# Attention and a feed-forward net side by side on one core: the first values in seven products, weight sums and the first rotation on GpSimd

## Chip, core and metric

The kernel runs on one core of a Trainium2 chip. The metric is the device time of one execution in microseconds (us). Before the change the median of three runs is 2091.97 us (2091.55 to 2092.16). One execution was also recorded by the profiler; the times of single instructions below come from that one. The engines are called PE (TensorE's matmuls; PEld are its weight loads), DVE (VectorE), ACT (ScalarE), POOL (GpSimd) and SP (SyncE, which here only issues DMAs).

## The reference

Sixteen batches of 512 tokens with 256 features. Everything is float32.

```python
def attn(x, wq, wk, wv, wo):                    # x: (16, 512, 256), 8 heads of 128
    q = rope(jnp.einsum('bim,mhd->bhid', x, wq))
    k = rope(jnp.einsum('bim,mhd->bhid', x, wk))
    v = jnp.einsum('bim,mhd->bhid', x, wv)
    s = jnp.einsum('bhid,bhjd->bhij', q, k) / 128
    s = s - 1e30 * mask                         # mask: i < j
    p = jax.nn.softmax(s, axis=-1)
    return jnp.einsum('bhid,hdm->bim', jnp.einsum('bhij,bhjd->bhid', p, v), wo)

def ffn(x, k0, k1, k2, s0, s1, s2):             # weights are +1 or -1
    h = jnp.concatenate([x, -x], axis=-1)
    h = jax.nn.relu(s0 * conn_dense(k0, h)) * 2
    h = jax.nn.relu(s1 * conn_dense(k1, h)) * 2
    return s2 * conn_dense(k2, h)

xn = layernorm(x)
out = x + attn(xn, wq, wk, wv, wo) + ffn(xn, k0, k1, k2, s0, s1, s2)
```

`rope` turns each head's vector by an angle that grows with the position: with the vector's two halves a and b, it gives a cos - b sin and a sin + b cos.

## The kernel before

**Tiling.** A batch's normalized tokens lie transposed in SBUF (`xnT`: features on the partitions, in two chunks of 128; tokens along the row, in four blocks of 128). A projection to 512 tokens is therefore two matmuls of 128x512 per head, or, for the values, where tokens are the output's rows, four products of 128x256 for each block of 128 tokens and each group of four heads (`project_v_directly`, L383: the sum over the two feature chunks, for two halves of the columns). One float32 matmul appears in the trace as two matmul records and two weight loads.

**Seven products.** A product of a 2x2 block matrix with a 2x2 block matrix needs eight block products; the kernel does most projections with seven, by a scheme of Strassen's kind (`seven_products`, L427). The weights' blocks A11, A12, A21 and A22 lie in places of `w7_sb` (queries and keys) and `wv7_sb` (values), beside three sums S1, S2 and S4, which `sum_w7` (L687) makes in four subtractions, the last of which replaces A21. Before them `scale_w7` (L680) scales the four blocks; for the values that is one instruction, the negation of A22, since the other scales are 1. Sums of the tokens' blocks are in `tt` (`make_ts`, L363, four subtractions a batch). Of the seven products two go to a PSUM tile `pa`, then two to a PSUM tile `pb`. ACT copies pa to `ca` and pb to `cb` in SBUF. The fifth product adds to pa, ACT copies one half of that to `cu`, the sixth adds to pb, the seventh to pa. Three additions on DVE then give the four blocks of the result. The tiles pa and pb come from a pool of three PSUM tiles (`ps_mm`), which also serves the direct projections and the feed-forward net; a tile is free again when its last reader is done.

**Rotation.** `rotate` (L395) has ACT swap the two halves of a head's vector from PSUM or SBUF into `sw` (two copies of 64x512), DVE multiply the source by the cosine, and then `engine` multiply sw by the sine (L411) and add the two (L413). For head 0 that engine is DVE (L879), for all others GpSimd.

**Stages.** The order on PE, SP and GpSimd is the program's order. In the opening (L874 to L884) that holds for DVE and ACT too; later a scheduler orders these two. The opening: normalize the first batch from `x_first`, transpose it on PE, make `tt` and the net's scales (`make_scales`, whose last result `c_sb` scales the tokens in `split_xn`), project head 0's q and k directly, split the tokens into two rounded halves (`split_xn`, ACT makes xh, DVE makes xl), and turn the net's first weights from bits into numbers (`make_w0`, L221: ACT makes `kb`, DVE `w0_sb`, for two chunks). Then come 128 slots, one per batch and head, each with the scores and softmax of its head (`score_row`), the projection of the next head's q and k, the attention product of the head before (`attend`), and a part of the net. The first slot (`first_slot`, L711) projects the values of the first batch's heads 0 to 3 directly, then head 1's q and k directly, then alternates score rows of head 0 with tiles of the net's first layer (`ffn0`). The later slots of the first batch make the sums of weights for what follows, on GpSimd; in the slot of head 4 these are the sums for the values of heads 0 to 3 (L868), which the next batch is the first to use.

**Loads.** SP issues them: the first tokens, head 0 and 1's wq, the cosine, the first group of the value weights (`load_wv(0)`, two DMAs), the scales s, k0, and then the rest. ACT issues half of the first tokens, wk of heads 0 and 1, and the sine.

The lines around the first values:

```python
        project_v_directly(0, 0)                       # L713
        rest(project_qk_directly(1, nc.gpsimd))        # L714
```

Of the kernel before, what the change touches and what calls it, by code (L numbers as in the profile page):

```python
# [9 lines left out]
F32 = mybir.dt.float32  # L10
# [12 lines left out]
def kernel(  # L23
# [36 lines left out]
    nc = tc.nc  # L60
    P = 128
    B, T, M = x.shape
# [3 lines left out]
    NT = T // P  # L66
    NM = M // P
# [14 lines left out]
    ps_mm = ctx.enter_context(tc.tile_pool(name="ps_mm", bufs=3, space=bass.MemoryType.PSUM))  # L82
# [17 lines left out]
    def load_x_sum(b):  # L100

        t = xpool.tile([P, NT, M], F32, tag="x_sum", name=f"x_sum_{b}", bufs=1)
        nc.sync.dma_start(t, by_chunks(x, b))
        return t
# [12 lines left out]
    A11, A12, A21, S1, S2, A22, S4 = range(7)  # L117
    WQ0, WQ1, WK0, WK1 = A11, A12, A21, A22
    NG = HD // (VH * D)
    VN = VH * D // 2  # L120
    wv7_sb = wpool.tile([P, 7, NG, VN], F32, tag="wv7", name="wv7_sb")
# [131 lines left out]
    xns, zxs, bounces, xnTs, halves, tts = {}, {}, {}, {}, {}, {}  # L253
# [58 lines left out]
    def tokens(t, m):  # L312
        return t[:, :, m].rearrange("p i c a -> p i (c a)")
# [9 lines left out]
    def carry_xn_out(b):  # L323
        bounces[b] = carry_out(zxs.pop(b).rearrange("p j m c a -> p j (m c a)"), "bounce_x", b)
# [50 lines left out]
    vts, qks, probs, pTs, oTs = {}, {}, {}, {}, {}  # L375
# [4 lines left out]
    def new_v(b, gv):  # L380
        vts[b, gv] = work.tile([P, NT, VH * D], F32, tag="v", name=f"v_{b}_{gv}")

    def project_v_directly(b, gv):  # L383
        new_v(b, gv)
        for c in range(NT):
            pv = ps_mm.tile([P, T], F32, tag="mm", name=f"pv_{b}_{gv}_{c}")
            for i, places in enumerate(((A11, A12), (A21, A22))):
                for m in range(NM):
                    nc.tensor.matmul(  # L389
                        pv[:, ts(i, VN)], tokens(xnTs[b], m)[:, c], wv7_sb[:, places[m], gv],  # L390
                        start=(i == 0 and m == 0), stop=(m == NM - 1), skip_group_check=True,
                    )
            nc.scalar.copy(vts[b, gv][:, c, :], pv)

    def rotate(src, name, g, engine, scale=1.0):  # L395


        sw = work.tile([P, T], F32, tag="sw", name=f"sw{name}_{g}")
        rt = work.tile([P, T], F32, tag=f"{name}T", name=f"{name}T_{g}")
        for to, half in ((sw[0:HALF, :], src[HALF:D, :]), (sw[HALF:D, :], src[0:HALF, :])):  # L400
            if scale == 1.0:
                nc.scalar.copy(to, half)  # L402
            else:
                nc.scalar.mul(to, half, scale)
        if scale == 1.0:
            nc.vector.tensor_tensor(rt, src, cos_sb, ALU.mult)
        else:
            nc.vector.scalar_tensor_tensor(rt, src, scale, cos_sb, ALU.mult, ALU.mult)
        qks.setdefault(g, []).append(rt)
        yield  # L410
        engine.tensor_tensor(sw, sw, sin_sb, ALU.mult)  # L411
        yield
        engine.tensor_tensor(rt, rt, sw, ALU.add)  # L413

    def project_qk_directly(g, engine):

        for name, places, scale in (("q", (WQ0, WQ1), Q_SCALE), ("k", (WK0, WK1), K_SCALE)):
            pq = ps_mm.tile([P, T], F32, tag="mm", name=f"p{name}_{g}")
            for m in range(NM):
                nc.tensor.matmul(  # L420
                    pq, w7_sb[:, places[m], ts(g, D)], tokens(xnTs[0], m),
                    start=(m == 0), stop=(m == NM - 1),
                )
            rest(rotate(pq, name, g, engine, scale))
            yield
# [60 lines left out]
    def project_v(b, gv, t):  # L486


        if t == 0:
            new_v(b, gv)  # L490
        vt = vts[b, gv]

        def product(out_, place, right, **marks):
            nc.tensor.matmul(  # L494
                out_, right[:, t], wv7_sb[:, place, gv], skip_group_check=True, **marks
            )

        for sums in seven_products(f"v_{b}_{gv}_{t}", b, product):
            if sums is None:
                yield  # L500
        nc.vector.tensor_tensor(vt[:, t, :VN], *sums[0], ALU.add)
        nc.vector.tensor_tensor(vt[:, t + 2, :VN], *sums[1], ALU.add)
        nc.vector.tensor_tensor(vt[:, t : t + 3 : 2, VN:], *sums[2], ALU.add)
        yield
# [165 lines left out]
    def rest(*gens):  # L670
        for gen in gens:
            for _ in gen:
                pass
# [6 lines left out]
    def scale_w7(w, i, scale1, scale2, raised=None):  # L680


        place, scale = ((A22, -scale2), (A21, scale2), (A11, scale1), (A12, scale1))[i]
        if scale != 1.0:
            behind(nc.scalar.mul(w[place], w[place], scale), raised)

    def sum_w7(w, reduced=None, engine=nc.vector):  # L687
        for out_, a, c in (
            (S1, A21, A22), (S2, S1, A11), (S4, A12, S2), (A21, A11, A21)
        ):  # L690
            tied = reduced if engine is nc.vector else None
            behind(engine.tensor_tensor(w[out_], w[a], w[c], ALU.subtract), tied)  # L692

    def w7_qk(h0, h1):
        return [w7_sb[:, i, h0 * D : h1 * D] for i in range(7)]

    def scale_w7_qk(h0, h1, i, raised):
        scale_w7(w7_qk(h0, h1), i, Q_SCALE, K_SCALE, raised)
# [6 lines left out]
    def make_w7_v(gv, reduced, raised, engine):  # L705
        w = [wv7_sb[:, i, gv] for i in range(7)]
        for i in range(4):
            scale_w7(w, i, 1.0, 1.0, raised)
        sum_w7(w, reduced, engine)

    def first_slot():  # L711
        l0 = [ffn0(0, f) for f in range(NF0)]
        project_v_directly(0, 0)  # L713
        rest(project_qk_directly(1, nc.gpsimd))  # L714
        for ic in range(NT):
            reduced, raised = score_row(0, ic)
            scale_w7_qk(2, 4, ic, raised)
            rest(l0[ic])
        sum_w7(w7_qk(2, 4), reduced, nc.gpsimd)
        turn(0, reduced)  # L720
        rest(*l0[NT:])
        make_w1(0, reduced, raised)
        load_w1(0, 0)
        for gv in range(1, NG):
            make_w7_v(gv, reduced, raised, engine=nc.gpsimd)
# [98 lines left out]
    def slot(g):  # L824
        b, h = divmod(g, H)
        load_w1(b, h)
        if h == 3:
            x_sums[b] = load_x_sum(b)
        if b + 1 < B:
            if h == 4:  # L830
                carry_xn_out(b + 1)
            if h == 5:
                carry_xn_back(b + 1)
        qk = project_qk(g + 1) if g + 1 < N_SLOTS else iter(())
        tile = ffn1(b, h - 1)
        v = iter(())
        if h in (2, 3):
            v = project_v(b, 1, h - 2)
        elif h == H - 1 and b + 1 < B:
            v = project_v(b + 1, 0, 0)  # L840
        some(qk, 1)
        for ic in range(NT):
            reduced, raised = score_row(g, ic)
            between_rows(b, h, ic, reduced, raised)
            if ic == 0:
                some(qk, 1)
                rest(ffn2(b, h - 2))
                some(qk, 1)
            else:
                some(tile, 4)  # L850
                if ic > 1:
                    some(qk, 1)
            if ic == 2:
                some(v, 1)
        rest(qk)
        turn(g, reduced)
        some(v, 1)
        project_o(g - 2)
        rest(v)
        rest(tile)  # L860
        attend(g - 1)
        if b == 0:
            make_w1(h, reduced, raised)
        if g == 2:
            make_w7_qk(6, H, reduced, raised, engine=nc.gpsimd)
        elif g == 3:
            make_w7_qk(0, 2, reduced, raised, engine=nc.gpsimd)
        elif g == 4:  # L868
            make_w7_v(0, reduced, raised, engine=nc.gpsimd)

    E = mybir.EngineType
    with tc.manual_schedule(engines={E.PE, E.SP, E.Pool}):
        with tc.manual_schedule(engines={E.DVE, E.Activation}):
            layernorm(0, x_first)  # L874
            transpose_first_xn()
            for i in range(4):
                make_ts(0, i)
            make_scales()
            q = project_qk_directly(0, nc.vector)  # L879
            next(q)  # L880
            split_xn(0, 0)
            rest(q)
            split_xn(0, 1)
            make_w0()  # L884
        first_slot()
        for g in range(1, N_SLOTS + 2):
            (slot_of_head_0, slot_of_head_1, slot)[min(g % H, 2)](g)
# [52 lines left out]
```

## Time and profile before

| what | value |
|---|---|
| median of three runs | 2091.97 us |
| the profiled execution | 2090.79 us |
| its span, first to last instruction | 2089.0 us |
| granted PE clock, mean | 0.999 |
| instructions | 30263 |
| bytes moved by DMA | 284.33 MB, 136 GB/s |

How to read it: a line of the trace in order of time gives the start (us from the span's beginning), the duration, the engine, the line of the kernel, the operation, what it writes `<-` what it reads, the shapes, and how many neighbours of one kind are merged (x4). In square brackets stands how long the engine was idle before it, and which instruction released it. Merged rows of one engine can overlap the next row by a little, because the ends of instructions include the way through the pipeline. A table of stretches gives for each stretch its length, and after the comma the busy time of PE, PEld, DVE, ACT and POOL with the number of their instructions.

The chain of waits, followed back from the end, goes through these lines of PE for most of the span:

| line | what | share |
|---|---|---|
| L648 | second layer of the net | 22% |
| L594 | sums into the output | 16% |
| L549 | probabilities times values | 13% |
| L511 | scores | 13% |
| L470 | q and k in seven products | 18% |
| L494 | values in seven products | 9% |
| L389 | values directly (first slot only) | 0.3% |

### The profile page before, as it was taken

What the parts mean: (1) busy time and instruction counts of PE and PEld (TensorE: products, weight loads), DVE (VectorE), ACT (ScalarE), POOL (GpSimd) and SP (SyncE); (2) the same over time, 40 slices, a digit from 0 to 9 for tenths busy, and PEclk for the clock granted to TensorE, in tenths of its full rate; (3) what the DMA queues carried; (4) which work ended last, traced back from release to release, by engine and by line L of the source; (5) the groups of instructions that cost most, each with busy time, mean ns of one, the idle gap of its engine ahead of it and who ended that gap; (6) DMA issues with size and microseconds to landing.
All of it is one profiled execution on the core that took longest, in us unless ns stands there. A gap on an engine that the chain in (4) does not pass through costs nothing.

```text
span 2089.0 us, 30263 instructions
## 1 busy us (share of the span) xinstructions
PE 2075.7 (99%) x9856; PEld 1730.4 (83%) x9856; DVE 1402.0 (67%) x3653; ACT 1086.6 (52%) x2419; POOL 1020.2 (49%) x1088
## 2 busy tenths in 40 slices
PE   8999999999999999999999999999999999999999
PEld 6888888888888888888888888888888888888887
DVE  7767666676766766667676676766667666676654
ACT  6655554555545555455554555555555554555543
POOL 5754545445454454444544455444544545545443
PEclk9999999999999999999999999999999999999999
DMA  6543545445444344543435444454453544534344
GB/s 182 164 145 118 159 116 147 132 123 149 126 144 136 122 138 126 149 139 119 146 114 163 125 136 135 120 159 116 137 151 112 152 116 141 157 117 137 106 139 129
DMA packets 162158, 284.33 MB, mean 136 GB/s; under 512 B 25168, under 2 KB 126544, under 8 KB 162000
## 3 DMA queue, kind: packets, MB, share of 16 engines
q1 hardware_dynamic: 160976, 281.34, 45.6%
q8 instruction: 78, 1.28, 0.3%
q10 hardware_dynamic: 1024, 1.05, 0.2%
q14 instruction: 80, 0.66, 0.1%
HBM read 178.00 MB, written 104.33 MB: 135 GB/s over the span
## 4 chain that ended last, share of the span: by engine, by line
PE 98%; DVE 1%; POOL 0%; issue 0%; ACT 0%; DMA 0%; POOLq 0%; DVEq 0%; ACTq 0%
PE ph L648 22%; PE y L594 16%; PE po L549 13%; PE s L511 13%; PE pa_qk L470 10%; PE pb_qk L470 8%; PE ph L633 6%; PE pa_v L494 5%; PE pb_v L494 4%; PE pv L389 0%; PE pq L420 0%; PE pk L420 0%; DVE p L514 0%; POOL w_sb L692 0%; DMA x_first<-in_L_attn_x_dram 0%
## 5 line engine op out<-in xcount | busy, mean ns | idle before, releaser
L522 POOL TENSOR_SCALAR p<-p,rl 128x128 f32<-128x128 f32 (+3 forms) x512 | 296.0, 583 | 733.2 <-DVE rl L521 730.0
L648 PE MATMUL ph<-h0h,w 128*128 128x512 f32 x1024 | 519.7, 507 | 0.0
L648 PE MATMUL ph<-h0l,w 128*128 128x512 f32 x1024 | 411.3, 402 | 0.0
L511 PE MATMUL s<-kT,qT 128*128 128x128 f32 (+3 forms) x1024 | 359.3, 432 | 0.2
L519 ACT ACTIVATE p<-p,least 128x128 f32<-128x128 f32 (+3 forms) x512 | 286.9, 561 | 123.6 <-DVE least L514 117.5
L411 POOL TENSOR_TENSOR swq<-swq,sin_sb 128x512 f32<-128x512 f32 x127 | 196.7, 1549 | 298.9 <-ACT swq L402 280.6
L530 DVE STREAM_TRANSPOSE z<-p 128x128 f32<-128x128 f32 (+3 forms) x512 | 241.8, 493 | 93.5 <-POOL p L522 89.8
L549 PEld LDWEIGHTS po<-pT,v 128*128 128x128 f32 x1536 | 271.1, 190 | 37.6
L549 PE MATMUL po<-pT,v 128*128 128x256 f32 (+1 forms) x1536 | 298.6, 344 | 0.0
L648 PEld LDWEIGHTS ph<-h0h,w 128*128 128x128 f32 x1024 | 193.1, 189 | 73.1 <-issue 26.9
L648 PEld LDWEIGHTS ph<-h0l,w 128*128 128x128 f32 x1024 | 193.3, 189 | 72.7 <-issue 26.8
L514 DVE CUSTOM_DVE_ANT_0 p<-s,causal 128x128 f32<-128x128 f32 (+3 forms) x512 | 244.2, 485 | 10.9 <-PE s L511 9.7
L402 ACT COPY swq<-q 64x512 f32<-64x512 f32 x252 | 156.3, 620 | 170.3 <-DVE q L480 168.9
L594 PE MATMUL y<-wo_sb,oT 128*128 128x256 f32 x1024 | 241.7, 379 | 0.0
L511 PEld LDWEIGHTS s<-kT,qT 128*128 128x128 f32 x1024 | 193.4, 189 | 33.6 <-POOL kT L413 0.5
L594 PEld LDWEIGHTS y<-wo_sb,oT 128*128 128x128 f32 x1024 | 193.9, 189 | 28.7
L445 ACT COPY ca_qk<-pa_qk 128x512 f32<-128x512 f32 x126 | 73.9, 587 | 275.2 <-PE pa_qk L470 275.2
L656 ACT ACTIVATE h1h<-ph 128x512 fp32r<-128x512 f32 x128 | 76.5, 597 | 250.7 <-PE ph L648 243.2
L521 DVE RECIPROCAL rl<-l 128x1 f32<-128x1 f32 x512 | 78.7, 154 | 145.5 <-ACT p L519 143.1
L413 POOL TENSOR_TENSOR kT<-kT,swk 128x512 f32<-128x512 f32 x127 | 169.2, 1332 | 0.1
L413 POOL TENSOR_TENSOR qT<-qT,swq 128x512 f32<-128x512 f32 x127 | 163.8, 1290 | 10.0
L411 POOL TENSOR_TENSOR swk<-swk,sin_sb 128x512 f32<-128x512 f32 x127 | 166.3, 1309 | 0.0
(107 smaller groups left out, 3497.9 us busy)
## 6 DMA issues: line engine op xcount, KB each, us to landing
bounce_p<-z SPq DMA_DIRECT2D x128, 640.0 KB, 2.9
pT<-bounce_p SPq DMA_DIRECT2D x512, 160.0 KB, 3.3
w<-w_dram SPq DMA_DIRECT2D x120, 512.0 KB, 5.2
x_sum<-in_L_attn_x_dram SPq DMA_DIRECT2D x16, 512.0 KB, 6.0
x<-in_L_attn_x_dram SPq DMA_DIRECT2D x60, 128.0 KB, 6.1
bounce_x<-zx SPq DMA_DIRECT2D x15, 512.0 KB, 6.7
xnT<-bounce_x SPq DMA_DIRECT2D x60, 128.0 KB, 5.9
out_dram<-x_sum SPq DMA_DIRECT2D x15, 512.0 KB, 4.5
```

What stands on the lines that cost most here:

```text
L411: engine.tensor_tensor(sw, sw, sin_sb, ALU.mult)
L413: engine.tensor_tensor(rt, rt, sw, ALU.add)
L470: nc.tensor.matmul(out_, w7_sb[:, place, ts(h, D)], right, skip_group_check=True, **marks)
L494: nc.tensor.matmul(out_, right[:, t], wv7_sb[:, place, gv], skip_group_check=True, **marks)
L511: nc.tensor.matmul(ps[:, :n], qT[:, ts(ic, P)], kT[:, :n], start=True, stop=True)
L514: reduced = nc.vector.tensor_tensor_reduce(out=p, in0=ps[:, :n], in1=causal[:, T - n :], scale=1.0, scalar=3e38, op0=ALU.add, op1=ALU.min, ...
L519: raised = nc.scalar.activation(p, p, AF.Exp, bias=least, scale=-1.0, accum_out=l)
L522: nc.gpsimd.tensor_scalar(p, p, rl, 1.0, ALU.mult, ALU.mult)
L530: behind(nc.vector.transpose(zs[:, :, block(ic, 0) : block(ic + 1, 0), :].rearrange("p j c a -> p c j a"), p.rearrange("p (c j a) -> p c j ...
L549: nc.tensor.matmul(po[:, (ics[0] - first) * P : (ics[-1] + 1 - first) * P], v[:, jc], pT[:, :, at[0] : at[-1] + 1 : max(at[-1] - at[0], 1) ...
L594: nc.tensor.matmul(ys[b][c // 2][:, c % 2, :], lhsT[:, ts(c, P)], rhs, start=(y_done[b][c] == 0 and c % 2 == 0), stop=(y_done[b][c] == N_Y ...
L648: nc.tensor.matmul(ph, w1s[b, f][:, c], h0s[b][i][:, c, :], start=(c == 0 and i == 0), stop=(c == NF0 - 1 and i == 1),)
```

## The change

The first batch's values of heads 0 to 3 are computed by `project_v`, in seven products for each half of the token blocks (t = 0: blocks 0 and 2; t = 1: blocks 1 and 3), as all other values are; `project_v_directly` is gone. The direct projection of head 1 is split: its q is projected between the two halves, its k after them. The scaled block and the sums of these value weights are made in the opening, after `make_scales`, with the four subtractions on GpSimd, and not in the slot of head 4. The two multiplications and two additions of head 0's rotation go from DVE to GpSimd, where they stand behind the sums.

```diff
-    def project_v_directly(b, gv):
-        new_v(b, gv)
-        for c in range(NT):
-            pv = ps_mm.tile([P, T], F32, tag="mm", name=f"pv_{b}_{gv}_{c}")
-            for i, places in enumerate(((A11, A12), (A21, A22))):
-                for m in range(NM):
-                    nc.tensor.matmul(
-                        pv[:, ts(i, VN)], tokens(xnTs[b], m)[:, c], wv7_sb[:, places[m], gv],
-                        start=(i == 0 and m == 0), stop=(m == NM - 1), skip_group_check=True,
-                    )
-            nc.scalar.copy(vts[b, gv][:, c, :], pv)
...
     def first_slot():
         l0 = [ffn0(0, f) for f in range(NF0)]
-        project_v_directly(0, 0)
-        rest(project_qk_directly(1, nc.gpsimd))
+        rest(project_v(0, 0, 0))
+        qk = project_qk_directly(1, nc.gpsimd)
+        next(qk)
+        rest(project_v(0, 0, 1), qk)
...
         elif g == 3:
             make_w7_qk(0, 2, reduced, raised, engine=nc.gpsimd)
-        elif g == 4:
-            make_w7_v(0, reduced, raised, engine=nc.gpsimd)
...
             make_scales()
-            q = project_qk_directly(0, nc.vector)
+            make_w7_v(0, None, None, engine=nc.gpsimd)
+            q = project_qk_directly(0, nc.gpsimd)
             next(q)
             split_xn(0, 0)
             rest(q)
```

`project_v`, which the first slot now calls, stood in the kernel before for the other values:

```python
    def project_v(b, gv, t):
        if t == 0:
            new_v(b, gv)
        vt = vts[b, gv]

        def product(out_, place, right, **marks):
            nc.tensor.matmul(
                out_, right[:, t], wv7_sb[:, place, gv], skip_group_check=True, **marks
            )

        for sums in seven_products(f"v_{b}_{gv}_{t}", b, product):
            if sums is None:
                yield
        nc.vector.tensor_tensor(vt[:, t, :VN], *sums[0], ALU.add)
        nc.vector.tensor_tensor(vt[:, t + 2, :VN], *sums[1], ALU.add)
        nc.vector.tensor_tensor(vt[:, t : t + 3 : 2, VN:], *sums[2], ALU.add)
        yield
```

In the changed kernel lines after L379 have smaller numbers: the copies ca, cb and cu are L433, L437 and L441, the three additions L489 to L491, the rotation's lines L390 to L401.

## The prediction

> **What bounds the kernel now.** I read the page's busy shares and its chain of waits first, then the first 31 us in order of time, because the change lies there, and last the busy time of stretches further on, to see what a shift at the start would meet.
>
> ```profile
> PE 2075.7 (99%) x9856; PEld 1730.4 (83%) x9856; DVE 1402.0 (67%) x3653; ACT 1086.6 (52%) x2419; POOL 1020.2 (49%) x1088
> ...
> PE 98%; DVE 1%; POOL 0%; issue 0%; ACT 0%; DMA 0%; POOLq 0%; DVEq 0%; ACTq 0%
> ```
>
> PE is busy for all but 13.3 us, 8.8 of them before the first projection, and the chain lies on PE for 98%. What PE loses or saves therefore reaches the end unless a later wait of PE takes it up. In order of time (start, duration, engine, line):
>
> ```profile
> 8.79 3.24 PE L420 MATMUL pq<-xnT,w_sb 128*128 128x512 f32 x4 [0.36 <-DVE xnT L341]
> ...
> 11.86 1.88 PE L420 MATMUL pk<-xnT,w_sb 128*128 128x512 f32 x4
> ...
> 13.58 7.07 PE L389 MATMUL pv<-wv_sb,xnT 128*128 128x256 f32 x32
> ...
> 15.88 2.17 ACT L224 ACTIVATE kb<-k_sb,sg_sb 128x1024 f32<-128x1024 uint8 x2
> ...
> 17.96 1.58 ACT L393 COPY v<-pv 128x512 f32<-128x512 f32 x3
> 18.47 2.47 DVE L225 SCALAR_TENSOR_TENSOR w_sb<-k_sb,sg_sb,kb 128x1024 fp32r<-128x1024 uint8 x2
> ...
> 20.48 1.88 PE L420 MATMUL pq<-xnT,w_sb 128*128 128x512 f32 x4
> ...
> 23.92 0.38 PE L511 MATMUL s<-kT,qT 128*128 128x128 f32 x2
> ```
>
> From 8.79 to 23.92 PE never stands still. The 16 direct products of the values (two records each) leave PE free at 20.48: 6.9 us, 0.432 each. They wait for nothing but a free PSUM buffer, so it does no harm that ACT starts the first copy of them only at 17.96, after both kb.
>
> **Removed and added on PE.** Out go 16 products of 128x256, in come two times seven: 14 x 0.432 = 6.05 against 6.91 us, **-0.86**.
>
> **The new waits of PE, first token half (t = 0).** The seven products are a chain through ACT: the fifth (S2) adds to pa only when ACT has copied pa away (ca), the sixth needs cb, the seventh needs cu. In the built kernel ACT's order is: negated A22, both swq, xh, both swk, xh, both kb, and only then ca, cb, cu. The fourth product has been issued at 13.58 + 4 x 0.432 = 15.31. ca is queued behind the kb pair, which nothing later needs before ffn0, and so starts no earlier than the copy of before, 17.96. It takes 0.59 (the ca copy at L445); from the end of such a copy to the matmul it frees, before has 0.14 (cu ends 37.98, PE goes on 38.12). PE goes on at 17.96 + 0.59 + 0.14 = 18.69: a stall of **3.38**. The fifth product takes 0.67 until its end (x2 at 38.12), cu 0.35 (L453), with 0.04 and 0.14 between them: 1.20, where PE has only 0.86 of work: **0.34**, and 0.08 because the restarted product takes 0.51 until the next can start.
>
> **Second half (t = 1).** pq of head 1 (1.72) lies between the halves. ACT takes its two swq first (1.20, L404), 0.07 after its end. PE needs from the start of pq to the sixth later slot 1.72 + 1.73 = 3.45; ca is done 1.88 + 0.07 + 1.20 + 0.59 = 3.74 after that start, with 0.14 to PE: 3.88, a stall of 0.43, less an overlap of some 0.05 of the copies: **0.4**. Then cu again: **0.34 + 0.08**. Sum of the four waits: 3.38 + 0.42 + 0.40 + 0.42 = 4.62; with -0.86 the first score starts **3.76** late.
>
> **The sums of the weights on GpSimd.** The two value loads are issued at 3.5 and 4.0 and land 6.5 to 6.8 later, by 10.8:
>
> ```profile
> L151 SPq DMA_DIRECT2D wv_sb<-in_L_attn_wv_dram x2: 379/721/1063, 3.5 to 4.0; - x2
> ...
> DMA to landing us min/median/max: 6.5/6.6/6.8
> ```
>
> The negation takes 0.41 on ACT (the later one of wv at 32.32), done at 11.2, while ACT has nothing to do until swq at 12.06: the cover is 0.85, and each later us of the load would shift swq, xh and kb by the same. The four sums take 3.2 to 3.5 (POOL at 94.95 and 34.72), from 11.25 to some 14.4. S1 is needed by PE's third product at 14.44 and is there at 12.0. But VectorE makes the scales then (11.69 to 12.91), three of its small instructions with two inputs in SBUF, and such instructions and those of GpSimd hold each other up:
>
> ```profile
> 39.80 1.29 POOL L411 TENSOR_TENSOR swq<-swq,sin_sb 128x512 f32<-128x512 f32 x1 [1.26 <-DVE k L482]
> ...
> 40.01 1.62 DVE L406 TENSOR_TENSOR kT<-k,cos_sb 128x512 f32<-128x512 f32 x1
> ...
> 41.17 1.61 POOL L413 TENSOR_TENSOR qT<-qT,swq 128x512 f32<-128x512 f32 x1
> ```
>
> kT, 0.68 alone, took 1.62: it stood until POOL's instruction ended at 41.09. If c_sb (L219) has to let the third sum end first, at 13.65, it is ready at 13.85 and ACT's xh starts 0.6 after its 13.28; swk, xh, kb and ca follow in order. Bounds: 0 (the small ones slip between two sums) and 1.35 (c_sb after the fourth sum). I take **+0.6**, worked out from the starts above.
>
> **The rotation of head 0 on GpSimd.** VectorE loses four instructions of 0.69, GpSimd gains four of 1.29 (23.72 to 28.98, with 1.37 from one to the next): 5.3 us from about 15, so 20.5 alone. The score that needs kT comes at 28, and swq of head 1 needs GpSimd only at 23: alone it costs nothing; without that cover every us over 7.5 would. Its danger is on VectorE: xl twice and w0 twice have both inputs in SBUF and meet it. Where both wanted the port (131.69 to 133.24), a waiting VectorE instruction went ahead of GpSimd's next, and the next VectorE one too. By that rule xl ends at 17.4, w0 waits for the qT add until 18.7 and ends at 21.15, and the three adds of the first half at 22.5; the second half's pa, which needs pa's buffer back, wants to start at 22.7. **0**, with 0 and 2.4 as bounds: the 2.4 if GpSimd's two last rotations (1.29 each) come in between.
>
> **Head 4 and later.** Four sums and a negation leave the slot of head 4. PE lost nothing to them, so **0**, and below zero nothing either: the stretch 93 to 107 has PE busy 14.00 of 14 us. No DMA is issued, moved or dropped; SP's and GpSimd's queues keep their order, the value loads being first in any case.
>
> **The sum.** 3.76 + 0.6 = **+4.4 us**. Against the profiled execution: 2090.79 + 4.4 = 2095.2 (its span 2089.0 and 1.8 around it). That execution was 1.18 under the median of the runs shown; against the median it is 2091.97 + 4.4 = **2096.4**.
>
> **What a pause does to PE's clock.** The first pq took 3.24 for four records, the next pk 1.88: after the start PE ran at half pace until about 11.8. Pauses up to 0.58 (58.60) did not bring this back, the standstill before 6.17 had it. The new pause, 4.0, lies between and is a little nearer to 6.17; yet the records of the start do not say that a pause in the middle does it. Price: 3.0 us at half pace (8.79 to 11.8) cost 1.5; counted from the transposes at 6.17, 5.6 us cost 2.8.
>
> The Trainium skill ("TensorE: Matmul & The Clock Gate", Part 1) speaks against this change: it says that PE falls back to half clock after a window of about 3.4 us without work, and that the windows run free of the program. No row of this trace shows such a fall. By that rule a pause of 4 us holds a whole idle window only at some phases; where it strikes, one window at half pace costs 1.7 us (an estimate from that page), and the sum by it would be 6.1 instead of 4.4.
>
> **Rivals.**
> (A) The forecast, own range +3.0 to +6.5 (2095.0 to 2098.5): 0.52.
> (B) The clock falls in the pause: 4.4 + 1.5 to 2.8, 2097.9 to 2099.2. For it the length of the pause, against it that no pause within this trace shows it and that part of the slow stretch would lie in waits on ACT anyway: 0.26.
> (C) GpSimd and VectorE take turns, and pa of the second half waits 2.4 for the adds: 2098.8. For it the row of 40.01, against it that of 131.69: 0.09.
> (D) Not slower: later waits take up the delay.
>
> ```profile
> 30.00:40.00 10.00, 9.11 (x39) 6.53 (x38) 9.64 (x22) 7.26 (x17) 7.89 (x12) 1.00 0.51 139
> 40.00:50.00 10.00, 9.89 (x48) 7.80 (x47) 8.90 (x26) 7.53 (x17) 9.41 (x9) 1.00 0.40 127
> 50.00:60.00 10.00, 9.31 (x40) 6.67 (x39) 6.75 (x18) 5.55 (x14) 7.79 (x10) 1.00 0.52 144
> ```
>
> The first figure after the comma is PE: it idles 0.89 + 0.11 + 0.69 = 1.7 us here. If these waits hung on GpSimd's or VectorE's backlog and not on PE's own products, they would vanish: +2.7, 2094.7, within 0.2%. It decides from the point where more than 0.2 of the 4.4 is taken up. Against it: the engines that set them are fed by PE's own later products: 0.08.
> (E) The copies are not held behind kb and the stalls stay under 0.9: 2091.1 to 2092. Against it ACT's order: 0.03.
>
> 0.2% (4.2 us) is about what a measurement of this kernel can tell from no change. Of A, 0.22 lies under it and 0.30 over it. Slower: 0.30 + 0.26 + 0.09 = 0.65; same: 0.22 + 0.08 + 0.03 = 0.33; faster by 4.2 needs more than the 0.86 saved and all 1.7 of D: 0.02. Range: 2094.6 (D) to 2100.2 (B with 1 us of C); about two in ten lie outside.
>
> **What would show it.** Right: ca (L433 of the changed kernel) starts straight after kb, near 18.6; PE idle some 3.9 before the fifth product, released by ca; the first score near 28.3. B: records of pq of head 1 at 0.8 instead of 0.43. C: pa of the second half released by the third of VectorE's adds (L491 of the changed kernel). The 0.6: xh at 13.9 and c_sb late. Wrong altogether: ca before kb, or a first score before 25.

## The result and the profile after

| | before | changed |
|---|---|---|
| median | 2092.0 us (8 runs, 2091.0 to 2092.8) | 2097.4 us (8 runs, 2097.1 to 2099.5) |
| the profiled execution | 2090.79 us | 2097.17 us |
| its span | 2089.0 us | 2095.4 us |

The change costs 5.4 us: the ratio is 1.0029, with a 95% interval of 1.002 to 1.0038. The forecast was 2096.4, its range 2094.6 to 2100.2.

The busy shares and the chain of waits of the changed kernel's page:

```profile
PE 2078.8 (99%) x9852; PEld 1733.4 (83%) x9852; DVE 1405.3 (67%) x3655; ACT 1085.6 (52%) x2421; POOL 1026.9 (49%) x1092
...
PE 97%; DVE 1%; DMA 0%; POOL 0%; ACT 0%; issue 0%; ACTq 0%; DVEq 0%; POOLq 0%
```

PE has four records fewer and is busy 3.1 us longer. A record is as long as PE's clock makes it, and its modelled end can cover a short wait: busy time alone does not tell work from slowness. The rest is idle time: 2095.4 - 2078.8 = 16.6 us, where there were 13.3. The opening of the changed kernel in order of time (start, duration, engine, line; in brackets the idle time before, and its releaser):

```profile
8.75 3.78 PE L408 MATMUL pq<-xnT,w_sb 128*128 128x512 f32 x4 [0.36 <-DVE xnT L341]
...
14.39 0.72 ACT L352 ACTIVATE xh<-xnT,c_sb 128x512 fp32r<-128x512 f32 x1 [0.63 <-DVE c_sb L219]
...
14.61 1.03 PE L482 MATMUL pa_v<-wv_sb,xnT 128*128 128x256 f32 x4
...
15.47 1.03 PE L482 MATMUL pb_v<-wv_sb,tt 128*128 128x256 f32 x4
...
16.98 2.17 ACT L224 ACTIVATE kb<-k_sb,sg_sb 128x1024 f32<-128x1024 uint8 x2
...
18.15 4.12 DVE L225 SCALAR_TENSOR_TENSOR w_sb<-k_sb,sg_sb,kb 128x1024 fp32r<-128x1024 uint8 x2 [0.29 <-ACT kb L224]
19.06 0.56 ACT L433 COPY ca_v<-pa_v 128x512 f32<-128x512 f32 x1
...
19.77 0.69 PE L482 MATMUL pa_v<-wv_sb,tt 128*128 128x256 f32 x2 [3.27 <-ACT ca_v L433]
...
22.06 2.70 PE L408 MATMUL pq<-xnT,w_sb 128*128 128x512 f32 x4
...
30.15 0.38 PE L499 MATMUL s<-kT,qT 128*128 128x128 f32 x2
```

ca starts as kb ends, and PE stands for 3.27 us until ca has emptied pa. Then two things are to be seen that the sum of the forecast did not have. The four records of pq after the pause take 2.70, against 1.88 for the same four before the change. And the first pq takes 3.78 and not 3.24, so that the value products begin at 14.61 and not at 13.58; up to there PE has the same work in both kernels, and in the six other kernels below without warming products they begin anywhere from 13.54 to 14.80. That part is scatter between executions.

The clock that PE was granted tells what the pause did. Stretches of 2 us; after the comma the busy time of PE, PEld, DVE, ACT and POOL, then PE's clock, the DMA share and GB/s:

```profile
18.00:20.00 2.00, 0.23 (x1) 0.26 (x2) 1.85 (x2) 2.00 (x4) 1.92 (x2) 1.00 1.14 305
20.00:22.00 2.00, 2.00 (x6) 1.41 (x6) 2.00 (x2) 0.48 (x2) 1.19 (x1) 0.57 1.12 216
22.00:24.00 2.00, 2.00 (x4) 0.87 (x3) 1.54 (x4) 0.00 (x0) 0.00 (x0) 0.58 1.12 246
24.00:26.00 2.00, 2.00 (x9) 1.44 (x8) 0.00 (x0) 1.11 (x2) 0.00 (x0) 1.00 1.11 314
```

The clock is below 1.00 in two stretches: 0.43 and 0.42 of 2 us are missing, and at half pace (0.50 in stretches of 1 us) that is (0.43 + 0.42) x 2 / 0.5 = 3.4 us of slow PE, right behind the pause.

Nothing later takes the delay up. In the chain of waits of the changed kernel, the first two of the pieces that come once in each batch (start, duration):

```profile
150.59 3.73 PE ph L636 x16
...
279.79 3.72 PE ph L636 x16
```

and the same of the kernel before:

```profile
144.27 3.73 PE ph L648 x16
...
273.47 3.72 PE ph L648 x16
```

The first score is 6.23 us late (30.15 against 23.92), this piece 6.32, and the next batch takes 129.20 us in both. The whole difference arises before the first score. It is 0.9 more than the medians show, because the two executions also differ by their starts. So the stretch from the first value product to the first score is the better measure; the table shows it for every kernel with direct projections in this place, beside the medians.

| kernel | first value product | first score | stretch | more than before | medians, this - before |
|---|---|---|---|---|---|
| before | 13.58 | 23.92 | 10.34 | | |
| changed | 14.61 | 30.15 | 15.54 | +5.20 | +5.4 |
| e1_copies_first | 14.47 | 26.26 | 11.79 | +1.45 | +1.4 |
| e2_pause_filled | 13.69 | 28.29 | 14.60 | +4.26 | +4.5 |
| e10_pause_shorter | 14.80 | 30.31 | 15.51 | +5.17 | +6.2 |
| e3_rotation_dve | 13.79 | 31.17 | 17.38 | +7.04 | +6.0 |
| e8_scales_first | 13.89 | 29.30 | 15.41 | +5.07 | +5.9 |
| e5_gpsimd_alone | 13.54 | 24.64 | 11.10 | +0.76 | -0.2 |
| e4_before_warm | 12.19 | 22.71 | 10.52 | +0.18 | -1.3 |
| e12_before_warm_scales | 12.16 | 22.50 | 10.34 | 0.00 | -1.7 |

The two with "warm" start the value products 1.4 us sooner, which the stretch leaves out.

### The profile page after: what moved, and what is told of

It is laid out like the page before. It is cut to its first block, busy times and chain, and to the rows that moved or that the text cites. A ratio compares the mean times of both kernels' runs of the same rounds, so it can differ in the third digit from the quotient of the medians.

```text
span 2095.4 us, 30273 instructions
## 1 busy us (share of the span) xinstructions
PE 2078.8 (99%) x9852; PEld 1733.4 (83%) x9852; DVE 1405.3 (67%) x3655; ACT 1085.6 (52%) x2421; POOL 1026.9 (49%) x1092
## 3 DMA queue, kind: packets, MB, share of 16 engines
q10 hardware_dynamic: 1024, 1.05, 0.2%
## 4 chain that ended last, share of the span: by engine, by line
PE 97%; DVE 1%; DMA 0%; POOL 0%; ACT 0%; issue 0%; ACTq 0%; DVEq 0%; POOLq 0%
PE ph L636 22%; PE y L582 16%; PE po L537 13%; PE s L499 13%; PE pa_qk L458 10%; PE pb_qk L458 8%; PE ph L621 6%; PE pa_v L482 5%; PE pb_v L482 4%; DMA w_sb<-in_L_attn_wk_dram 0%; DVE p L502 0%; DMA s_sb<-in_L_ffn_s_dram 0%; POOL w_sb L680 0%; PE pq L408 0%; POOL swk L399 0%
## 5 line engine op out<-in xcount | busy, mean ns | idle before, releaser
L390 ACT COPY swq<-q 64x512 f32<-64x512 f32 x252 | 155.9, 619 | 171.0 <-DVE q L468 169.5
L433 ACT COPY ca_qk<-pa_qk 128x512 f32<-128x512 f32 x126 | 73.7, 585 | 275.7 <-PE pa_qk L458 275.7
L401 POOL TENSOR_TENSOR kT<-kT,swk 128x512 f32<-128x512 f32 x128 | 171.5, 1340 | 0.2
L401 POOL TENSOR_TENSOR qT<-qT,swq 128x512 f32<-128x512 f32 x128 | 165.4, 1292 | 10.0
```

## The experiments

Theory: the copy ca, queued behind kb, makes the loss; a part of it is what the pause does to PE's clock. Rivals: GpSimd's and VectorE's new work makes it, or the clock has no part. Each difference is between two medians taken on the same chip; in brackets stands the 95% interval of the ratio. Whether the clock held is read from each kernel's profiled execution.

**e1_copies_first: the first half's copies ahead of kb.**

```diff
             split_xn(0, 1)
+            rest(project_v(0, 0, 0))
             make_w0()
...
-        rest(project_v(0, 0, 0))
         qk = project_qk_directly(1, nc.gpsimd)
```

> The changed kernel with the first half's values (their seven products, the copies ca, cb, cu and the three adds) put ahead of make_w0 in the opening, so that ACT copies before both kb. Theory 1 (ACT's kb pair ahead of ca makes PE's pause, and the pause lets PE's clock fall): ca starts near 16.5 to 17, PE's pause shrinks from 3.3 to 1 to 1.5, the records after it run at full pace; 3.0 to 3.6 us less than the changed kernel, 2093.8 to 2094.4. Rival (the port shared by GpSimd and VectorE makes the loss: late c_sb, slow w0): those stay as they are, so at most 0.6 less, 2096.8.

Measured: 2092.93 against 2091.51, +1.4, ratio 1.0008 [0.9999 to 1.0016]. In order of time:

```profile
15.33 1.03 PE L482 MATMUL pb_v<-wv_sb,tt 128*128 128x256 f32 x4
...
16.55 0.56 ACT L433 COPY ca_v<-pa_v 128x512 f32<-128x512 f32 x1
...
17.26 0.67 PE L482 MATMUL pa_v<-wv_sb,tt 128*128 128x256 f32 x2 [0.90 <-ACT ca_v L433]
...
18.23 2.19 ACT L224 ACTIVATE kb<-k_sb,sg_sb 128x1024 f32<-128x1024 uint8 x2
...
18.99 1.88 PE L408 MATMUL pq<-xnT,w_sb 128*128 128x512 f32 x4
...
26.26 0.38 PE L499 MATMUL s<-kT,qT 128*128 128x128 f32 x2
```

ca goes ahead of kb, the pause shrinks from 3.27 to 0.90, and pq keeps full pace. Four of the 5.4 us are gone with one line moved (3.0 to 3.6 were expected), while the sums, the rotation and the seven products are all still there. The order on ACT makes the loss. That 1.4 are left is no riddle. The seven products save 0.86. The fifth product could have started at 15.33 + 0.86 = 16.19 and started at 17.26, a loss of 1.07 (the 0.90 in brackets leaves out modelled ends). The three shorter waits for the copies were put at 0.42 + 0.40 + 0.42 = 1.24. Together that is +1.45, what the table has. At this place they cost more in waits than they save, even in a better order; by the medians alone this stays just short of shown, since the interval reaches 1.

**e2_pause_filled: the same order, PE kept busy in the pause** with three products that nothing reads.

```diff
-        rest(project_v(0, 0, 0))
+        v = project_v(0, 0, 0)
+        next(v)
+        idle = ps_t.tile([P, T], F32, tag="t", name="idle")
+        for i in range(3):
+            nc.tensor.matmul(
+                idle, tokens(xnTs[0], 0)[:, 0], tokens(xnTs[0], i % 2),
+                start=(i == 0), stop=(i == 2),
+            )
+        rest(v)
```

> The changed kernel with three products of 128x512 that nobody reads put behind the fourth of the first half's seven products, 2.6 us of work in the pause of 3.3 (the result is as before). Theory of the clock (it falls because PE stands still): the pause is no window without work any more, the sixth and seventh product and q of head 1 run at 0.43 per record; 1.0 to 1.4 us less, 2096.0 to 2096.4. Rival (the slow records there have another cause, such as the same instructions waiting for operands): no less, or up to 0.5 more.

Measured: 2095.97 against 2091.51, +4.5, ratio 1.0021 [1.0012 to 1.0029]; all 11 runs (to 2096.52) lie below all 8 of the changed kernel (from 2097.13), but those were not taken beside them, and the intervals of the two ratios overlap. In order of time:

```profile
15.56 2.74 PE L705 MATMUL idle<-xnT 128*128 128x512 f32 x6
19.29 0.67 PE L482 MATMUL pa_v<-wv_sb,tt 128*128 128x256 f32 x2 [0.99 <-ACT ca_v L433]
...
21.02 1.88 PE L408 MATMUL pq<-xnT,w_sb 128*128 128x512 f32 x4
...
28.29 0.38 PE L499 MATMUL s<-kT,qT 128*128 128x128 f32 x2
```

and two of its stretches, as above:

```profile
20.00:22.00 2.00, 1.93 (x7) 1.03 (x7) 2.00 (x2) 0.37 (x1) 0.72 (x1) 1.00 1.15 202
22.00:24.00 2.00, 2.00 (x9) 1.39 (x8) 1.07 (x3) 0.97 (x2) 0.00 (x0) 1.00 1.10 244
```

PE waits for ca just as long, yet the clock stays at 1.00 and pq takes 1.88. From the fifth product to the first score it is 28.29 - 19.29 = 9.00 us here (and in e1_copies_first, 26.26 - 17.26), against 30.15 - 19.77 = 10.38 in the changed kernel: the lost clock cost 1.38 us in that execution. By the medians it is 0.9.

**e10_pause_shorter: one unread product in place of three,** to see how short a pause can be and still cost the clock.

```diff
-        for i in range(3):
-            nc.tensor.matmul(
-                idle, tokens(xnTs[0], 0)[:, 0], tokens(xnTs[0], i % 2),
-                start=(i == 0), stop=(i == 2),
-            )
+        nc.tensor.matmul(
+            idle, tokens(xnTs[0], 0)[:, 0], tokens(xnTs[0], 0), start=True, stop=True
+        )
```

(against e2_pause_filled)

> The changed kernel with one unread product of 128x512 (0.86 us) in the pause, which leaves some 2.4 to 2.6 us of it. If the clock falls only after a full window of some 3.4 us without work: no fall, as with three products, +4.4 to +4.7 over the kernel before. If a window that is mostly without work is enough: a fall in many executions, +5.0 to +5.6.

Measured: 2097.55 against 2091.33, +6.2, ratio 1.0028 [1.0017 to 1.004]. In order of time:

```profile
19.82 0.67 PE L482 MATMUL pa_v<-wv_sb,tt 128*128 128x256 f32 x2 [2.27 <-ACT ca_v L433]
```

and its stretches:

```profile
20.00:22.00 2.00, 2.00 (x6) 1.22 (x6) 2.00 (x2) 0.53 (x2) 1.25 (x1) 0.66 1.14 202
22.00:24.00 2.00, 2.00 (x4) 0.93 (x3) 1.60 (x4) 0.00 (x0) 0.00 (x0) 0.50 1.12 230
24.00:26.00 2.00, 2.00 (x8) 1.39 (x8) 0.00 (x0) 0.95 (x2) 0.00 (x0) 0.99 1.12 333
```

A pause of 2.27 us loses the clock too, again for (0.34 + 0.50 + 0.01) x 2 / 0.5 = 3.4 us. The theory that a longer pause is needed falls. (The time lies above the +5.0 to +5.6 expected for this case, and it scatters from 2095.6 to 2098.5; more on that below.) The Trainium skill ("TensorE: Matmul & The Clock Gate", Part 1) has the clock fall after an idle window of about 3.4 us; a pause of 2.27 us holds no such window, so here the measurement decides against that threshold, while the 3.4 us of slow PE fit the length that the page gives to one window.

**e3_rotation_dve: head 0's rotation back on VectorE.**

```diff
-            q = project_qk_directly(0, nc.gpsimd)
+            q = project_qk_directly(0, nc.vector)
```

> The changed kernel with head 0's rotation back on VectorE (the sums stay on GpSimd). Theory 1 (the pause of PE makes the loss, the rotation's place costs nothing): ca starts as late as in the changed kernel, since only the sums make c_sb late; w0 takes 2.5 us again instead of 4.1, but VectorE has four instructions more before it; +5.0 to +6.2 over the kernel before. Rival (GpSimd's rotation holds VectorE up and with it PE): 1.5 us less than the changed kernel, +3.9.

Measured: 2097.29 against 2091.33, +6.0, ratio 1.0027 [1.0017 to 1.0038]: as slow as the change. In order of time:

```profile
19.35 2.47 DVE L225 SCALAR_TENSOR_TENSOR w_sb<-k_sb,sg_sb,kb 128x1024 fp32r<-128x1024 uint8 x2
...
19.68 1.19 PE L482 MATMUL pa_v<-wv_sb,tt 128*128 128x256 f32 x2 [3.57 <-ACT ca_v L433]
```

The two L225 take 2.47 again and not 4.12, so GpSimd and VectorE did collide there, but nothing on PE waited for it. In this execution the pause was 3.57 and the clock stayed low for twice as long: the stretches of 2 us from 18 to 26 miss 0.34, 0.50, 0.50 and 0.36 of full pace, (0.34 + 0.50 + 0.50 + 0.36) x 2 / 0.5 = 6.8 us. That, and a longer pause, make the largest stretch of the table.

**e5_gpsimd_alone: the kernel before, with the change's work on GpSimd** (the negation, four subtractions that nothing reads, head 0's rotation), the values still direct.

```diff
-            q = project_qk_directly(0, nc.vector)
+            u = [wv7_sb[:, i, 0] for i in range(7)]
+            nc.scalar.mul(u[S4], u[A22], -1.0)
+            for o, a, c in ((S1, A21, S4), (S2, S1, A11), (S4, A12, S2), (S1, A11, A21)):
+                nc.gpsimd.tensor_tensor(u[o], u[a], u[c], ALU.subtract)
+            q = project_qk_directly(0, nc.gpsimd)
```

> The kernel before (values direct) with only the GpSimd part of the change: one negation on ACT and four subtractions of the same size at the same place, written to places that nobody reads before the slot of head 4 makes the real sums, and head 0's rotation on GpSimd. Theory 1: the port makes c_sb some 0.6 to 1.1 late and ACT's copies of the values with it, PE waits as long for a free PSUM tile; 0.4 to 1.1 more than before, 2092.4 to 2093.1. Rival (the port makes most of the loss): 3 us more or above, 2095 and up.

Measured: 2091.29 against 2091.51, -0.2, ratio 0.9997 [0.9988 to 1.0005]. In order of time:

```profile
14.09 0.72 ACT L352 ACTIVATE xh<-xnT,c_sb 128x512 fp32r<-128x512 f32 x1 [0.88 <-DVE c_sb L219]
...
19.38 1.99 PE L389 MATMUL pv<-wv_sb,xnT 128*128 128x256 f32 x8 [0.50 <-ACT v L393]
```

The late c_sb is there, and with direct products it shows on PE as 0.50 before the fourth tile. The +0.4 to +1.1 expected did not show in the medians; a loss of that size cannot be told from none there. That GpSimd's part alone makes a loss of several us is refuted.

**e8_scales_first: the changed kernel with the loads of s issued by ACT, ahead of the sine,** so that VectorE's scales are made before the sums begin.

```diff
-    for i, s in enumerate((s0, s1, s2)):
-        nc.sync.dma_start(s_sb[:, i : i + 1], s.partition_broadcast(P))
...
     nc.sync.dma_start(cos_sb, cos_t)
+    for i, s in enumerate((s0, s1, s2)):
+        nc.scalar.dma_start(s_sb[:, i : i + 1], s.partition_broadcast(P))
     nc.scalar.dma_start(sin_sb, sin_t)
```

> The changed kernel with the three tiny loads of the scales issued by ACT ahead of the sine, so that they land sooner and VectorE has made c_sb before GpSimd's sums begin. Theory (the sums hold up VectorE's small instructions, these c_sb, this ACT's xh and all behind it up to ca): the small instructions take 0.16 each again, xh starts straight after swq, ca 0.5 to 0.9 earlier, 0.4 to 0.9 less than the changed kernel: +4.5 to +5.0 over the kernel before. Rival (c_sb's lateness is taken up elsewhere): no less than the changed kernel's +5.4.

Measured: 2097.21 against 2091.33, +5.9, ratio 1.0027 [1.0016 to 1.0037]. Three of VectorE's small instructions, first in the changed kernel, where the sums run from 11.33 to 14.34:

```profile
11.33 3.01 POOL L680 TENSOR_TENSOR wv_sb<-wv_sb 128x256 f32<-128x256 f32 x4 [4.66 <-ACT wv_sb L673]
...
11.48 0.59 DVE L212 TENSOR_SCALAR neg<-s_sb 128x3 f32<-128x3 f32 x1 [1.19 <-DMA s_sb<-in_L_ffn_s_dram]
...
12.18 0.69 DVE L214 TENSOR_TENSOR sg_sb<-sg_sb,neg 128x3 f32<-128x3 f32 x1
...
14.03 0.33 DVE L219 TENSOR_TENSOR c_sb<-c_sb,ab_sb 128x1 f32<-128x1 f32 x1
```

then in e8_scales_first, where they come before the sums:

```profile
10.12 0.16 DVE L212 TENSOR_SCALAR neg<-s_sb 128x3 f32<-128x3 f32 x1
...
10.39 0.16 DVE L214 TENSOR_TENSOR sg_sb<-sg_sb,neg 128x3 f32<-128x3 f32 x1
...
11.17 0.16 DVE L219 TENSOR_TENSOR c_sb<-c_sb,ab_sb 128x1 f32<-128x1 f32 x1
```

The hold-up by GpSimd is real, and it is gone here: xh follows swq at once, and from the start of swq to ca it is 18.27 - 12.37 = 5.90, against 19.06 - 12.57 = 6.49. ca is 0.6 earlier, as the forecast's term says. But the pause of 3.20 still cost the clock, and the time shows none of the 0.4 to 0.9 expected: the term's worth in time stays open.

**e4_before_warm and e12_before_warm_scales: the kernel before with a full pace from the start.** Sixteen unread products of the identity lie ahead of the transposes, where PE waits for the first tokens; e12 also has the loads of e8_scales_first.

```diff
+            warm = ps_t.tile([P, T], F32, tag="t", name="warm")
+            for i in range(16):
+                nc.tensor.matmul(
+                    warm[:, ts(i % NT, P)], ident, ident, start=(i == 0), stop=(i == 15),
+                    skip_group_check=True,
+                )
             transpose_first_xn()
```

> The kernel before with sixteen transposing-size products of 128x128 on the unit matrix ahead of the first transposes, while PE has nothing else to do (1.7 to 6.2 us); nobody reads them. Theory of the clock (PE starts slow and needs some 3.4 us of work to run at full pace): the first projections run at 0.43 per record instead of 0.86 from 8.8 to 11.8; 1.0 to 1.7 us less than before, 2090.3 to 2091.0, and less spread between runs. Rival (the first projections are slow for another reason, such as loads still landing in the same memory): no change.

> The kernel before (values direct) with the warming products and the same early loads of the scales. Theory (direct products need none of ACT's copies, so only the warming counts): -1.2 to -1.6 against the kernel before, as with the warming alone (-1.3) or 0.2 better, and better than the seven products in any order tried. Rival (the warming's gain was chance): within 0.4 of the kernel before.

Measured: 2090.24 against 2091.51 (-1.3, ratio 0.9993 [0.9984 to 1.0002]) and 2090.03 against 2091.72 (-1.7, ratio 0.9993 [0.9984 to 1.0002]). e4_before_warm in order of time:

```profile
1.67 5.21 PE L877 MATMUL warm<-ident 128*128 128x128 f32 x32 [1.67 <-POOL ident masks.py:199]
...
8.65 1.98 PE L420 MATMUL pq<-xnT,w_sb 128*128 128x512 f32 x4 [0.57 <-DVE xnT L341]
...
22.71 0.39 PE L511 MATMUL s<-kT,qT 128*128 128x128 f32 x2
```

The first pq takes 1.98 and not 3.24. These are the lowest medians of all, but each interval just reaches 1: a gain is likely and not shown.

**e7_reordered_warm and e11_reordered_warm_scales: the changed kernel in the best order that the other runs suggested,** with warm; e11 also with the loads of e8_scales_first.

```diff
             q = project_qk_directly(0, nc.gpsimd)
-            next(q)
-            split_xn(0, 0)
             rest(q)
-            split_xn(0, 1)
+            rest(project_v(0, 0, 0))
+            for m in range(NM):
+                split_xn(0, m)
             make_w0()
...
-        rest(project_v(0, 0, 0))
+        v = project_v(0, 0, 1)
+        next(v)
         qk = project_qk_directly(1, nc.gpsimd)
         next(qk)
-        rest(project_v(0, 0, 1), qk)
+        next(v)
+        next(qk)
+        rest(v, qk)
```

(`project_qk_directly` also yields between its products and its rotation.)

> A version meant to beat both: the changed kernel with the first half's products, copies and adds ahead of the splitting of the tokens and of make_w0, with q of head 1 between the fourth and fifth product of the second half (its swap behind cu), and with the sixteen warming products ahead of the first transposes. Theory (only the order of ACT's work made the seven products lose): no pause above 0.7 us, full pace throughout; -0.2 to -0.9 against the kernel before, that is within 1.1 of the kernel before with the warming products alone (-1.3). Rival (the chain through ACT costs too much in any order): +1.5 or more over the warmed kernel before.

> The reordered and warmed seven products with the loads of the scales issued by ACT ahead of the sine. In the reordered kernel PE waited 1.5 us for pb's PSUM tile, that is for qT on VectorE, which stood behind c_sb, which GpSimd's sums had held up. Theory (the port's hold on the small instructions comes out on PE once the opening is quick): that wait goes, 1.0 to 1.5 us less than the reordered kernel's +0.8, so -0.2 to -0.7 against the kernel before. Rival (another wait takes its place): +0.5 or more.

Measured: 2092.09 against 2091.33 (+0.8, ratio 1.0005 [0.9996 to 1.0014]) and 2094.87 against 2091.72 (+3.2, ratio 1.0015 [1.0006 to 1.0023]). Both missed the gain, and in both it was the rival's case that came (e7 lies 2.1 above the warmed kernel before, e11 above +0.5). In e7 a wait came first that the old order had hidden, for the rotation of head 0 behind the held-up scales:

```profile
14.97 1.10 PE L483 MATMUL pb_v<-wv_sb,tt 128*128 128x256 f32 x4 [1.50 <-DVE qT L396]
```

e11 takes that wait down to 0.17, and gets a longer one:

```profile
17.91 3.48 DVE L353 SCALAR_TENSOR_TENSOR xl<-xnT,c_sb,xh 128x512 fp32r<-128x512 f32 x2
...
19.24 1.60 POOL L401 TENSOR_TENSOR kT<-kT,swk 128x512 f32<-128x512 f32 x1
...
21.32 3.51 DVE L225 SCALAR_TENSOR_TENSOR w_sb<-k_sb,sg_sb,kb 128x1024 fp32r<-128x1024 uint8 x2
...
25.55 3.78 PE L408 MATMUL pk<-xnT,w_sb 128*128 128x512 f32 x4 [3.00 <-DVE v L491]
```

xl and w0 are held up by GpSimd's rotation, VectorE's additions for the values come after them, PE waits 3.00 for these, and the clock goes as well: pk takes 3.78 for what takes 1.88. The first of its slow stretches:

```profile
24.00:26.00 2.00, 0.45 (x1) 0.45 (x2) 2.00 (x4) 0.00 (x0) 0.00 (x0) 0.55 1.11 307
```

The four stretches from 24 to 32 miss 0.45, 0.50, 0.50 and 0.26 of full pace: 1.71 x 2 / 0.5 = 6.8 us. No version with seven products here beat the kernel before.

## Why the prediction was right, and what it left out

**The shift reaches the end: right.** 6.23 us at the first score, 6.32 at 150 us, the same 129.20 for the batch after, 6.4 at the end of the span. Rival D, later waits that take it up, is refuted.

**ca behind kb: right, in place and length.** From swq to ca ACT took 6.49 us; the forecast has 18.56 - 12.06 = 6.50. The pause itself, from the time at which the fifth product could have started (15.47 + 0.86 = 16.33) to 19.77, was 3.44 against 3.98 forecast: ACT came 0.50 late, PE 1.02, both by the slower start of this execution. Rival E (copies not held behind kb) did not occur; made on purpose, as e1_copies_first, it measured 2092.9, above the 2091.1 to 2092 that it was given.

**The 0.86 saved and the three small waits: right.** From the fifth product to the first score the forecast has 27.68 - 18.69 = 8.99; where the clock held, it was 9.00.

**c_sb 0.6 late: the number by luck.** The term had c_sb wait for the third sum. It waited for the fourth: three of VectorE's small instructions, two of them with one input, each stood until a sum ended, and c_sb came at 14.36, the last sum ending at 14.34. In front of xh that shows as 0.63 only because swq was 0.51 late here; in e5_gpsimd_alone it is 0.88, in e2_pause_filled 0.97. All lie within the bounds of 0 and 1.35. Its share of the time could not be told.

**Rotation and head 4 at nothing: right in the cost, not in the working.** e3_rotation_dve is no faster. But the rule read at 131.69, that VectorE goes ahead of GpSimd's next instruction, did not hold: the engines took turns. The first w0 ended at 20.07, GpSimd's kT at 21.19, the second w0 at 22.27, where the working had 21.15; L225 took 4.12 for 2.47. The adds still came in time (the last ends at 23.54, PE takes pa of the second half at 24.60; in e2_pause_filled, where the clock held, the add that frees its buffer ended at 22.47 and PE came at 22.74, so only 0.27 to spare). So the turns of rival C came, and its wait of 2.4 did not; in e11_reordered_warm_scales, where the adds stand behind xl and w0 and PE comes sooner, the wait came too.

**What the pause does to PE's clock: the step that failed.** The forecast saw the mechanism, gave it 0.26 as rival B and nothing in the sum, because no pause of the trace showed it. It happened: 1.38 us in the profiled execution, a little under the 1.5 to 2.8 given, as a part of the slow stretch lies in the wait for cu. In the traces of five kernels a pause of 2.27 us or more lost the clock every time; after pauses of 0.90, 0.99 and, in e7_reordered_warm, 1.50 it held. The error was to count a fall as nothing in the sum until a trace showed one: the longest pause that had proved harmless was 0.58, the new one 4.0, and a pause seven times as long should have had the larger chance.

For the stretch from first value product to first score the account closes: forecast +4.36; the pause 0.54 shorter; the clock +1.38; together +5.20, measured +5.20. By the medians, +4.4 was forecast, +5.4 came, and +4.5 came where the clock held. That the time lies inside the own range of A, the forecast, although what came is the mechanism of rival B, is partly luck: the pause was shorter and the fall cheaper than either gave it.

Whether a fall comes in every execution can be read in part from the mean clock on record for each run, given to three places. A mean of 1.000 over 2095 us leaves room for some 1.05 us of missing clock (an estimate, 0.0005 x 2095), and 3.4 us at half pace miss 1.7. So the two runs of e10_pause_shorter at 1.000 (2095.56 and 2096.81, of six) and the two of e11_reordered_warm_scales (2093.27 and 2093.71, its fastest of eleven) had no such fall; whether their pause was shorter is not recorded. Of the changed kernel's eight runs none is at 1.000. A mean of 0.999 proves nothing, as many runs of the kernel before have it.

What stays open: what decides whether a pause costs the clock. Its length alone is not shown to: the pauses that did and did not lie apart in these traces (2.27 and more, 1.50 and less), but in e11 the clock fell at 24.2, only 1.7 us after PE had stopped at 22.55.

## What to carry to other kernels

Before a scheme that saves products is put on a critical stretch, count what each of its steps waits for on other engines, and what stands in their queues ahead of it: here seven products saved 0.86 us, and the waits for their copies cost 1.07 + 1.24 = 2.3 in the better order and 3.44 + 1.24 = 4.7 behind two unrelated instructions. Charge a PE pause of 2.3 us or more for its length and, as a likely extra, for a slow stretch after it: 1.3 to 2.5 us in the traces here. Put the copy that ends the pause ahead of work that nobody waits for (4.0 of the 5.4 us here); filling the pause with unread work kept the clock, but gave only 0.9 by the medians.

## What the hardware showed beyond that

- The slow stretch came in units, each worked out from the granted clock as above: 3.4 us with pauses of 2.27, 3.20 and 3.27, but 6.8 with 3.57 and with 3.00 (e11), so the length of the pause does not order them. What does order them in these five traces is when the clock fell (read from stretches of 0.25 us): 0.8 and 0.5 after PE had gone on (e10 and the changed kernel) and 0.1 before it (e8) gave one unit, 1.05 and 1.35 before it (e3 and e11) gave two. A unit cost 1.3 to 1.5 us from the fifth product to the first score, as part of it lies in other waits; two cost 2.5 in e3.
- Three of VectorE's six instructions on 128x3 numbers, 0.16 us alone, took 0.59 to 0.70 beside GpSimd's subtractions, each until a subtraction ended; the other three fell into the gaps between two subtractions and took 0.15 to 0.17. The Trainium skill ("SBUF — State Buffer", Who interferes with whom) says that whoever comes first holds the shared ports for a whole instruction; the trace agrees, and shows that a very small instruction waits out a long one in full.
- The start of the first value product scattered by 1.3 us (13.54 to 14.80) over eight executions with the same work of PE up to there, because the first projections were slow for a shorter or longer time. The row of the granted clock reads 1.00 there, although a record of the first pq takes twice its later time: it does not show the slow start. With sixteen unread products ahead of them they began at full pace.
